# Two attention layers on one core: their chunks taken in turns, scores in groups of three, projections in 64x64 tiles

## The chip, the cores and the metric

The kernel runs on one core of one Trainium2 chip. The time is the device time of one execution, in microseconds (us); the kernel before takes 3326.32 us (median of 3 runs, 3324.19 to 3328.06).

## The reference

Eight images of 64 channels and 64 x 64 = 4096 positions go through two self-attention layers. Everything is fp32.

```python
# layer 0 (f and g have 8 channels, hh has 64)
f, g, hh = Wf @ xf + bf, Wg @ xf + bg, Wh @ xf + bh
s = jnp.einsum('bci,bcj->bij', f, g)
o = jnp.einsum('bcj,bij->bci', hh, jax.nn.softmax(s, axis=2))
x = x + o
# layer 1 (64 channels, one head)
xn = group_norm(x, 8 groups, gamma, beta)
q, k, v = split(w_qkv @ xn + b_qkv)
attn = softmax(einsum('bqc,bkc->bqk', q, k) * 64**-0.5)
out = w_proj @ (attn @ v) + b_proj + x
```

## The kernel before

An image is held as 128 partitions (64 channels of each half of the positions) by 2048 columns. An attention is worked in four **chunks** of 512 query columns, and a chunk in 16 **steps**. A step has two **blocks**: the scores of one block go into a score buffer in PSUM (there are three), the exponential takes them to SBUF, and the weighting matmuls of the step before add to an accumulator. VectorE sums the exponentials for the softmax denominator.

```python
for s in range(nsteps):                      # 4 chunks x 16 steps, one image, one layer
    for p in range(2):                       # two blocks
        ps = ps_s.tile([P, 2, CW], F32, tag="s", ...)      # 3 buffers
        for h in range(2):
            at.scores(ps[:, h, :], t, p, h, c)
    ...
        nc.scalar.activation(e[:, p], pss[p], AF.Exp, scale=at.scale)
    if ready is not None:
        weigh(*ready)                        # the step before
    ... units of the next attention's projections, finishing of the last chunk
```

The weighting of layer 0: two matmuls, one for each half `h`, use 128 rows and 64 columns of the array each. (In the trace each of these fp32 matmuls stands as two instructions: 4096 for 2048 calls. "Instructions" below are those of the trace.)

```python
# Layer0
def weigh(self, acc, e, t, p, start, stop):
    for h in range(2):
        nc.tensor.matmul(
            acc[0][ts(h, C), :], self.vt[:, p, t, :], e[:, h, :], start=start, stop=stop)
```

Layer 1 uses four 64x64 tiles at once for scores and weighting. The projections of layer 0 (f, g) and layer 1 (q, k) are full-width matmuls with zero or repeated weights. Attentions follow each other whole: layer 0 of image b, then layer 1 of image b-1.

Of the kernel before, what the change touches and what calls it, by code (L numbers as in the profile page):

```python
# [68 lines left out]
def fast_path(  # L69
# [13 lines left out]

    nc = tc.nc
# [9 lines left out]
    xpool = ctx.enter_context(tc.tile_pool(name="xpool", bufs=4))  # L94
    proj = ctx.enter_context(tc.tile_pool(name="proj", bufs=2))
    ppool = ctx.enter_context(tc.tile_pool(name="ppool", bufs=6))
# [23 lines left out]
    def zeros(name):  # L120
        t = const.tile([P, P], F32, name=name)
        nc.vector.memset(t, 0.0)
        return t
# [9 lines left out]
    wf, wg = zeros("wf"), zeros("wg")  # L133
    fb = const.tile([P, 1], F32, name="fb")
    gb = const.tile([P, 1], F32, name="gb")

    lane = const.tile([P, 1], I32, name="lane")
    nc.gpsimd.iota(lane, pattern=[[0, 1]], base=0, channel_multiplier=1)

    def low_rows(name, bit):  # L140
        hit = const.tile([P, 1], I32, name=f"{name}_bit")
        nc.vector.tensor_single_scalar(hit, lane, bit, op=ALU.bitwise_and)
        t = const.tile([P, 1], F32, name=name)
        nc.vector.tensor_scalar(t, hit, -1.0 / bit, None, op0=ALU.mult)
        return t

    fmask, gmask = low_rows("fmask", 2 * C8), low_rows("gmask", C8)
    for h in range(2):
        for p in range(2):
            r = 2 * h + p  # L150
            for j in range(4):
                rows = ds(32 * r + C8 * j, C8)
                nc.sync.dma_start(wf[ts(h, C), rows], WfT)
                nc.scalar.dma_start(wg[ts(p, C), rows], WgT)
                nc.gpsimd.dma_start(fb[rows, :], column(bf))
                nc.gpsimd.dma_start(gb[rows, :], column(bg))
    wh = diagonal("wh", WhT)
    hb = both("hb", bh)
    load_x(1)
# [3 lines left out]
    ones = const.tile([P, C], F32, name="ones")  # L163
# [4 lines left out]
    for h in range(2):  # L168
# [13 lines left out]
    stash = const.tile([P, 2 * B * NC * 2 * CW // P], F32, name="stash")  # L182
    recips = [
        dram.tile([P, 2 * CW // P], F32, name=f"recips_{i}") for i in range(2 * B * NC)
    ]

    def layer1_constants():


        wq = diagonal("wq", WqkvT[:, 0:C])  # L190
        wk = const.tile([P, 2, C], F32, name="wk")
        for p in range(2):
            for h in range(2):
                nc.gpsimd.dma_start(wk[ts(p, C), h, :], WqkvT[:, C : 2 * C])
        wp = diagonal("wp", WpT)
        wv = const.tile([C, C], F32, name="wv")
        nc.gpsimd.dma_start(wv, WqkvT[:, 2 * C : 3 * C])
        qb = both("qb", bqkv[0:C])
        kb = both("kb", bqkv[C : 2 * C])
        vb = both("vb", bqkv[2 * C : 3 * C])  # L200
        pb = both("pb", bp)
        gam = both("gam", gamma)
        bet = both("bet", beta)

        t0 = ps_s.tile([P, 2, CW], F32, tag="s", name="c_ps0")
        nc.tensor.transpose(t0[:C, 0, 0:C], wv, ident[0:C, 0:C])
        wvt = const.tile([C, 2, C], F32, name="wvt")
        for h in range(2):
            nc.vector.tensor_copy(wvt[:, h, :], t0[:C, 0, 0:C])
        t1 = ps_s.tile([P, 2, CW], F32, tag="s", name="c_ps1")  # L210
        nc.tensor.matmul(
            t1[:, 0, 0:C], wvt.rearrange("m h c -> m (h c)"), wp[0:C, 0:C], start=True, stop=True
        )
        wvp = zeros("wvp")
        for h in range(2):
            nc.vector.tensor_copy(wvp[ts(h, C), ts(h, C)], t1[ts(h, C), 0, 0:C])
        t2 = ps_s.tile([P, 2, CW], F32, tag="s", name="c_ps2")
        nc.tensor.matmul(t2[:, 0, 0:1], wvp, bet, start=True, stop=False)
        nc.tensor.matmul(t2[:, 0, 0:1], wp, vb, start=False, stop=True)
        nc.tensor.matmul(t2[:, 1, 0:1], wq, bet, start=True, stop=True)  # L220
        pbe = const.tile([P, 1], F32, name="pbe")
        nc.vector.tensor_add(pbe, t2[:, 0, 0:1], pb)
        qbe = const.tile([P, 1], F32, name="qbe")
        nc.vector.tensor_add(qbe, t2[:, 1, 0:1], qb)
        t3 = ps_s.tile([P, 2, CW], F32, tag="s", name="c_ps3")
        nc.tensor.matmul(
            t3[:, 0, 0:1], wk[0:C, :, :].rearrange("m h c -> m (h c)"), bet[0:C, :],
            start=True, stop=True,
        )
        kbe = const.tile([P, 1], F32, name="kbe")  # L230
        nc.vector.tensor_add(kbe, t3[:, 0, 0:1], kb)
        return wq, wk, gam, wvp, pbe, qbe, kbe


    def values(vt, src, w, c, name):

        ps = ps_s.tile([P, 2, CW], F32, tag="s", name=name)
        for t in range(TPC):
            nc.tensor.matmul(ps[:, 0, ts(t, P)], src[:, ts(t, P)], w, start=True, stop=True)  # L239
        nc.vector.tensor_copy(  # L240
            vt[:, :, ts(c, TPC), :],
            ps[:, 0, :].rearrange("k (t p c) -> k p t c", p=2, c=C),
        )

    class Attention:
        def __init__(self, index, b):
            self.index, self.b, self.name = index, b, f"l{self.kind}_{b}"

        def finish(self, acc, esum, c):

            n = f"{self.name}_{c}"
            raw = self.total(acc, n)
            zt = small.tile([P, 2 * CW // P], F32, tag="zt", name=f"zt_{n}")
            r = work.tile([P, CW], F32, tag="r", name=f"r_{n}")

            def sums():
                z = ps_s.tile([P, 2, CW], F32, tag="s", name=f"z_{n}")
                for h in range(2):
                    nc.tensor.matmul(  # L259
                        z[ts(h, C), 0, :], ones, esum[:, h, :], start=True, stop=True  # L260
                    )
                zs = work.tile([P, CW], F32, tag="zs", name=f"zs_{n}")
                nc.scalar.copy(zs, z[:, 0, :])  # L263
                for h in range(2):
                    nc.sync.dma_start(zt[ts(h, C), :], zs[h * C : h * C + 1, :])

            def reciprocals():
                dealt = recips[self.index * NC + c]
                rt = stash[:, ts(self.index * NC + c, 2 * CW // P)]
                nc.vector.reciprocal(rt, zt)  # L270
                nc.sync.dma_start(dealt, rt)
                for h in range(2):
                    row = dealt[ts(h, C), :].rearrange("p e -> (p e)")
                    nc.sync.dma_start(r[ts(h, C), :], row.partition_broadcast(C))

            def result():
                nc.vector.tensor_mul(raw, raw, r)  # L277
                self.residual(raw, c)

            return [(2, sums), (4, reciprocals), (8, result)]  # L280

    class Layer0(Attention):
        kind = 0
        banks = 1
        scale = 1.0

        def before(self):
            fg = proj.tile([P, 2, NH], F32R, tag="kfg", name=f"fg_{self.name}")
            self.f, self.g = fg[:, 0, :], fg[:, 1, :]
            self.vt = proj.tile([P, 2, NT, C], F32, tag="vt", name=f"vt_{self.name}")  # L290
            yield from (lambda c=c: self.project(c) for c in range(NC))

        def project(self, c):
            xc = x_tiles[self.b][:, ts(c, CW)]
            ps = ps_s.tile([P, 2, CW], F32, tag="s", name=f"fg_{self.name}_{c}")
            nc.tensor.matmul(ps[:, 0, :], wf, xc, start=True, stop=True)  # L296
            nc.tensor.matmul(ps[:, 1, :], wg, xc, start=True, stop=True)  # L297
            for i, (dst, bias, mask) in enumerate(((self.f, fb, fmask), (self.g, gb, gmask))):
                n = f"{i}_{self.name}_{c}"
                full = work.tile([P, CW], F32, tag="full", name=f"full{n}")  # L300
                nc.scalar.activation(full, ps[:, i, :], AF.Identity, bias=bias)  # L301
                high = work.tile([P, CW], F32R, tag="high", name=f"high{n}")
                nc.vector.tensor_copy(high, full)  # L303

                nc.vector.scalar_tensor_tensor(
                    dst[:, ts(c, CW)], high.bitcast(F32), mask, full,
                    op0=ALU.mult, op1=ALU.add,
                )
            values(self.vt, xc, wh, c, f"h_{self.name}_{c}")

        def scores(self, ps_ap, t, p, h, c):
            rows = ts(2 * h + p, 32)
            nc.tensor.matmul(  # L313
                ps_ap, self.g[rows, ts(t, P)], self.f[rows, ts(c, CW)], start=True, stop=True
            )

# [6 lines left out]
        def total(self, acc, n):  # L323
            raw = work.tile([P, CW], F32, tag="raw", name=f"raw_{n}")
            nc.scalar.copy(raw, acc[0])
# [565 lines left out]
```

## Time and profile before

| | before |
|---|---|
| median | 3326.32 us |
| TensorE busy | 3238.3 us, 97% |
| VectorE, ScalarE busy | 76%, 65% |
| an attention of layer 0, of layer 1 | 174, 236 us |
| first exponential starts | 43.67 us |

### The profile page before, as it was taken

How to read it: one execution, taken by the hardware profiler on the slowest of the kernel's cores; microseconds unless marked ns; L12 is line 12 of the kernel's file. 1: busy time of each engine (PE TensorE's matmuls, PEld its weight loads, DVE VectorE, ACT ScalarE, POOL GpSimd, SP SyncE). 2: the span in 40 equal slices, each digit the busy share in tenths (PEclk: the TensorE clock that was granted, in tenths of full speed). 3: DMA queues.
4: the chain of work that ended last, by engine and by line, in shares of the span. 5: the costliest groups of instructions: out<-in, count | busy, mean ns of one | idle time of the engine just before them, and what ended most of it. 6: DMA issues, size and time to landing. Idle time of an engine off the chain costs nothing.

```text
span 3324.7 us, 54178 instructions
## 1 busy us (share of the span) xinstructions
PE 3238.3 (97%) x23661; PEld 1109.9 (33%) x23661; DVE 2540.8 (76%) x1583; ACT 2170.2 (65%) x2329; POOL 33.2 (1%) x73
## 2 busy tenths in 40 slices
PE   6999999999999999999999999999999999999997
PEld 2323333333333333333333333332333323333332
DVE  5988866798667986678866798678876688766665
ACT  4778755687556765577655786557865577655554
POOL 3000000000000000000000000000000000000000
PEclk9999999999999999999999999999999999999999
DMA  2000000000000000000000000000000000000000
GB/s 54 7 7 7 8 7 11 23 7 7 8 14 20 7 8 7 14 20 7 8 8 14 23 4 7 12 9 10 7 4 14 8 10 7 4 14 7 14 8 15
DMA packets 42005, 37.90 MB, mean 11 GB/s; under 512 B 27248, under 2 KB 27424, under 8 KB 41760
## 3 DMA queue, kind: packets, MB, share of 16 engines
q1 hardware_dynamic: 38656, 34.14, 4.2%
q8 instruction: 187, 3.06, 0.4%
q0 software_dynamic: 1824, 0.19, 0.1%
q14 instruction: 58, 0.48, 0.0%
q10 hardware_dynamic: 1280, 0.03, 0.0%
HBM read 25.42 MB, written 8.65 MB: 10 GB/s over the span
## 4 chain that ended last, share of the span: by engine, by line
PE 82%; DVE 10%; DMA 3%; ACT 2%; issue 2%; POOL 1%; SPq 0%; DVEq 0%; ACTq 0%; POOLq 0%
PE s_l L391 27%; PE acc_l L399 26%; PE acc_l L319 19%; DVE esum_l L449 8%; PE s_l L313 5%; PE z_l L259 2%; ACT e_l L464 2%; DMA r_l<-recips 2%; DMA recips<-stash 1%; PE fg_l L296 1%; PE h_l L239 1%; PE fg_l L297 1%; PE k_l L379 1%; PE q_l L385 1%; PE v_l L239 0%
## 5 line engine op out<-in xcount | busy, mean ns | idle before, releaser
L464 ACT ACTIVATE e_l<-s_l 128x1024 f32<-128x1024 f32 x2048 | 1983.9, 1023 | 881.6 <-PE s_l L391 665.0
L449 DVE TENSOR_TENSOR esum_l<-esum_l,e_l 128x2048 f32<-128x2048 f32 x896 | 2051.6, 2290 | 414.4 <-ACT e_l L464 374.5
L319 PE MATMUL acc_l<-e_l,vt_l 128*64 128x512 f32 x4096 | 1010.4, 611 | 0.0
L391 PE MATMUL s_l<-q_l,k_l 64*64 64x512 f32 x8192 | 980.4, 591 | 0.0
L399 PE MATMUL acc_l<-e_l,vt_l 64*64 64x512 f32 x8192 | 976.4, 589 | 0.0
L399 PEld LDWEIGHTS acc_l<-e_l,vt_l 64*64 64x64 f32 x8192 | 318.4, 133 | 563.6 <-issue 454.7
L391 PEld LDWEIGHTS s_l<-q_l,k_l 64*64 64x64 f32 x8192 | 309.1, 133 | 566.0 <-issue 542.7
L319 PEld LDWEIGHTS acc_l<-e_l,vt_l 128*64 128x64 f32 x4096 | 252.4, 137 | 426.6 <-issue 410.7
L313 PE MATMUL s_l<-fg_l 32*128 32x512 f32 x2048 | 268.6, 499 | 17.5 <-ACT e_l L464 10.6
L313 PEld LDWEIGHTS s_l<-fg_l 32*128 32x128 f32 x2048 | 101.7, 183 | 412.6 <-issue 319.1
L449 DVE TENSOR_TENSOR esum_l<-e_l,e_l 128x2048 f32<-128x2048 f32 x64 | 146.7, 2291 | 76.8 <-ACT e_l L464 76.7
L277 DVE TENSOR_TENSOR raw_l<-raw_l,r_l 128x512 f32<-128x512 f32 x64 | 44.3, 693 | 122.6 <-DMA r_l<-recips 122.6
L263 ACT COPY zs_l<-z_l 128x512 f32<-128x512 f32 x64 | 37.5, 586 | 74.2 <-PE z_l L259 74.2
L451 DVE TENSOR_TENSOR esum_l<-esum_l 128x1024 f32<-128x1024 f32 x64 | 78.4, 1225 | 2.2
L259 PE MATMUL z_l<-esum_l,ones 128*64 128x512 f32 x256 | 67.9, 607 | 5.3 <-DVE esum_l L451 4.5
L270 DVE RECIPROCAL stash<-zt_l 128x8 f32<-128x8 f32 x64 | 12.8, 200 | 78.7 <-DMA zt_l<-zs_l 78.7
L301 ACT ACTIVATE full_l<-fg_l,fb 128x512 f32<-128x512 f32 x32 | 22.0, 687 | 77.7 <-PE fg_l L297 77.7
L303 DVE CAST high_l<-full_l 128x512 fp32r<-128x512 f32 x64 | 27.0, 422 | 41.1 <-ACT full_l L301 41.1
L383 ACT ACTIVATE k_l<-k_l,kbe 128x1024 f32<-128x1024 f32 x32 | 35.7, 1115 | 34.7 <-PE k_l L379 34.7
L296 PE MATMUL fg_l<-x,wf 128*128 128x512 f32 x64 | 36.6, 655 | 21.9 <-DMA wf<-in_WfT_dram 21.9
L409 DVE TENSOR_TENSOR raw_l<-acc_l,part_l 128x512 f32<-128x512 f32 x32 | 22.1, 690 | 25.6 <-ACT part_l L407 25.6
L407 ACT COPY part_l<-acc_l 128x512 f32<-128x512 f32 x32 | 18.7, 585 | 32.9 <-PE acc_l L399 32.9
(97 smaller groups left out, 629.2 us busy)
## 6 DMA issues: line engine op xcount, KB each, us to landing
r_l<-recips SPq DMA_DIRECT2D x128, 128.0 KB, 2.9
x<-in_x_dram SPq DMA_DIRECT2D x32, 256.0 KB, 4.9
out_dram<-raw_l SPq DMA_DIRECT2D x64, 128.0 KB, 2.4
zt_l<-zs_l SPq DMA_DIRECT2D x128, 2.0 KB, 1.8
recips<-stash SPq DMA_DIRECT2D x64, 4.0 KB, 1.4
wg<-in_WgT_dram ACTq DMA_DIRECT2D x16, 2.0 KB, 3.6
fb<-in_bf_dram POOLq DMA_DIRECT2D x16, 0.0 KB, 3.0
gb<-in_bg_dram POOLq DMA_DIRECT2D x16, 0.0 KB, 2.9
```

Of the source, the lines that this page charges most:

```text
L259: nc.tensor.matmul(z[ts(h, C), 0, :], ones, esum[:, h, :], start=True, stop=True)
L263: nc.scalar.copy(zs, z[:, 0, :])
L277: nc.vector.tensor_mul(raw, raw, r)
L296: nc.tensor.matmul(ps[:, 0, :], wf, xc, start=True, stop=True)
L313: nc.tensor.matmul(ps_ap, self.g[rows, ts(t, P)], self.f[rows, ts(c, CW)], start=True, stop=True)
L319: nc.tensor.matmul(acc[0][ts(h, C), :], self.vt[:, p, t, :], e[:, h, :], start=start, stop=stop)
L383: nc.scalar.activation(self.k[:, :, ts(c, CW)], ps, AF.Identity, bias=kbe)
L391: nc.tensor.matmul(ps_ap[ts(m, C), :], self.k[ts(h, C), p, ds(t * P + m * C, C)], self.q[ts(h, C), ts(c, CW)], start=True, stop=True,)
L399: nc.tensor.matmul(acc[m][ts(h, C), :], self.vt[ts(m, C), p, t, :], e[ts(m, C), h, :], start=start, stop=stop,)
L449: nc.vector.tensor_add(esum, first if t == 1 else esum, e)
L451: nc.vector.tensor_add(esum[:, 0], esum[:, 0], esum[:, 1])
L464: nc.scalar.activation(e[:, p], pss[p], AF.Exp, scale=at.scale)
```

## The change

The intent: relieve layer 0, where VectorE and TensorE are both nearly full, by letting its chunks alternate with those of layer 1; change tile shape less often (groups of three blocks); cut the cost of the projections; and start sooner. The diff, cut to its core:

```diff
+    lead = NC + 2                                  # six chunks of layer 0 first
+    seq = chunks0[:lead]
+    for i, one in enumerate(chunks1):              # then the layers take turns
+        seq.append(one)
+        seq.extend(chunks0[lead + i : lead + i + 1])
...
     class Layer0(Attention):
+        group = 3                                  # blocks scored together (Layer1: 2)
...
+            for j in range(2):                     # f and g of two chunks, 64x64 tiles
+                for h in range(2):
+                    nc.tensor.matmul(
+                        ps[ts(j, C), h, :], wfg[ts(h, C), :], xt[ts(h, C), ts(2 * k + j, CW)], ...)
+            # ... split in two parts, then 16 copies into the rows that the scores read
+                            nc.sync.dma_start(dst[rows, cols]..., split[...])
...
     class Layer0(Attention): def residual(self, o, c):
+            nc.vector.bn_stats(self.st[:, c, :], xc)        # statistics by chunk
...
     class Layer1(Attention): def before(self):
+            # steps of the chunk ahead of the image's first one
+            return [(0, channels), (2, means), (4, deviations), (6, begin)] + [
+                (6 + 2 * c, lambda c=c: self.project(c)) for c in range(1, NC)]
...
+            j = blocks[-1] + 1
+            now = i * NT + j // 2 - 1
+            run_until(now)                         # inserted work: row sums, projections, statistics
+            for r in ready:
+                weigh(*r, now)                     # weighting of the group before
```

Also in it: four loads of weights at the start in place of 32, layer 1's constants moved into the loop, the square root of the statistics by integer start value and four Newton steps on VectorE, row sums in four 128x32 tiles (which drops VectorE's half-sum), seven buffers of exponentials for six, three image buffers for four, one half of each key copied by DMA, and the finishing of a layer-0 chunk put off until the layer-1 chunk after it has run.

## The prediction

> **What bounds the kernel now.** I read the page's busy shares first, then two stage windows, then the order of time inside each stage, and the start last.
>
> The page puts TensorE at 97%, but the stages differ. In the busy times by stretch (us, busy of PE, weight loads, VectorE, ScalarE), the first row is one attention of layer 1, the second one of layer 0:
>
> ```profile
> PE 3238.3 (97%) x23661; PEld 1109.9 (33%) x23661; DVE 2540.8 (76%) x1583; ACT 2170.2 (65%) x2329; POOL 33.2 (1%) x73
> ...
> 1205.00:1441.00 236.00, 235.23 (x2108) 85.13 (x2100) 165.42 (x103) 133.23 (x143) 0.00 (x0) 1.00 0.04 9
> ...
> 1031.00:1205.00 174.00, 168.00 (x856) 52.80 (x858) 151.48 (x93) 137.77 (x148) 0.00 (x0) 0.99 0.06 15
> ```
>
> Layer 1 is solid TensorE, with VectorE idle for 71 us of 236. Layer 0 has TensorE and VectorE both nearly full. The timeline shows one step (two blocks of scores, their weighting) of layer 0 on TensorE, then its sums on VectorE:
>
> ```profile
> 1092.03 0.51 PE L313 MATMUL s_l<-fg_l 32*128 32x512 f32 x4
> 1092.47 1.94 PE L319 MATMUL acc_l<-e_l,vt_l 128*64 128x512 f32 x8
> ...
> 1094.34 0.50 PE L313 MATMUL s_l<-fg_l 32*128 32x512 f32 x4
> ...
> 1096.10 11.86 DVE L449 TENSOR_TENSOR esum_l<-esum_l,e_l 128x2048 f32<-128x2048 f32 x5
> ```
>
> A layer 0 step takes TensorE 2.30 us from start to start (0.44 scores, 1.87 weighting). Five sums take 11.86 us, one 2.29 (the page's mean), so they start (11.86 - 2.29) / 4 = 2.39 apart. Sixteen steps make a chunk: 38.3 us of VectorE for sums alone, 36.8 of TensorE. To this VectorE adds projections, statistics and residuals, 43 us in all per chunk, which is what a chunk takes (174 / 4 = 43.5). A layer 1 step (16 score and 16 weighting matmuls of 1.72 us each) takes 3.43, a chunk 54.9, and with projections and row sums 59 (236 / 4).
>
> The start, from the timeline and the chain: sixteen weight loads on each of two queues, then the projections, then layer 1's constants; the first score matmul comes at 42.8.
>
> ```profile
> 1.25 11.38 ACTq L154 DMA_DIRECT2D wg<-in_WgT_dram  x16
> ...
> 8.42 11.21 SPq L153 DMA_DIRECT2D wf<-in_WfT_dram  x16
> ...
> 21.85 2.05 PE L296 MATMUL fg_l<-x,wf 128*128 128x512 f32 x2 [21.85 <-DMA wf<-in_WfT_dram]
> ```
>
> I split TensorE's time into streaming and changes of tile shape. One pass of 512 columns takes 0.215 us, four passes for fp32, one for the rounded fp32 of layer 0's scores. In the program order of before I count 2966 us of streaming and 1195 changes of shape. From start to start a change costs 0.10 to 0.22 us: 8 weighting matmuls take 1.87 before scores, though 16 of the other layer stream for 1.72. The changes sum to 212. 2966 + 212 = 3178, less 11 at the start; the loop lasts 3324.7 - 42.8 - 19 (tail) = 3263. So about 97 us are stalls, 9 or 10 in each attention of layer 0 and under 1 in each of layer 1.
>
> **What the skill says.** The Trainium skill, "TensorEngine Tiling (Array Packing)", section Tiling Modes, says that a change of tiling mode (not of tile) drains TensorE; the 0.10 to 0.22 us above agree. Its page "ScalarE: Activation LUTs", section What ACT_TABLE_LOAD costs, gives about 1283 ns for a table load; the trace has 16 of 1283 ns in the loop, for the square root, 20.6 us of ScalarE. They go, but ScalarE is at 65%. "DMA: Bandwidth & Descriptors", section Rules for kernel authors, advises issuing a transfer early and waiting late; the copies of f, g and k do this, except at the start.
>
> **The change part by part.**
>
> *Projections in 64x64 tiles.* Before, f and g took 4 instructions of 0.43 us a chunk, 1.72; after, one group of four concurrent tiles (0.86) serves two chunks. 32 x (1.72 - 0.43) = 41 us. q and k go from 1.72 to 0.86: 32 x 0.86 = 27 us. Streaming falls by 69.
>
> *Groups of three.* Scores and weighting change shape 11 times a chunk, not 16. But a third block uses row groups that the first holds, so it can't run beside it. Where before had three blocks in a row, six matmuls took 0.73 us against 0.50 for four:
>
> ```profile
> 1030.82 0.73 PE L313 MATMUL s_l<-fg_l 32*128 32x512 f32 x6
> ```
>
> A group costs 0.65 + 2.58 + 0.15 = 3.38 us; ten and one group of two make 36.05 a chunk against 36.8. Over all: +34 us of streaming, fewer changes. In the order of after I count 1091 changes of all kinds, 179 us, and 2933 of streaming: 3112 against 3178. **TensorE's work falls by 66 us.**
>
> *Turns.* VectorE is what held layer 0, so its lag may now run into a layer 1 chunk, where it gains 1.04 us a step (3.43 - 2.39). Seven buffers of exponentials, of which the groups hold about three, allow some 10 us of lag. With both layers' finishing work (5.4 us) VectorE has 43.7 in a layer 0 chunk, TensorE 36.05 + 2.2 for row sums = 38.25: a lag of 5.5, which fits. A plain pair costs 38.25 + 55.2 + about 1 = 94.5.
>
> *Where turns don't help.* Six chunks of layer 0 come first, alone. VectorE holds them: 40.9 each, 48 with the next image's projection, 51 with layer 1's: 258 in all. And all of a layer 1 image's statistics and projections fall in one layer 0 chunk. There TensorE waits in order for the normalised x, which VectorE makes after six sums and some 30 small operations, near 24 us into the chunk; TensorE arrives near 20. Then queries, keys, values and scores share three score buffers, some 4 us more. I walk it to 54 us against 47.6 of TensorE's work. Six such chunks lie among the pairs: 6 x 15.75 = 94.5 above plain. Six layer 0 projections add 7.7 each, 46.
>
> *Start.* Four weight loads, not sixteen; layer 1's constants move into the loop. First matmul near 8.5, scaled copies to 13.7; six copies at some 0.57 us of issue (as two small loads take 1.15), plus 2.2 to land: first exponential near 20, not 43.7. A gain of 23.
>
> *Off the path.* The dropped half-sum (64 x 1.225 = 78 us) and the casts spare VectorE; layer 1's extra eviction costs ScalarE 32 x 0.585 = 19. Neither is a bound in a pair.
>
> *Sum.* 20 start + 258 lead + 26 x 94.5 = 2457 pairs + 94.5 + 46 + 347 for the last six layer 1 chunks (56.3 each, one image's projection 8, leftovers) + 19 tail = 3241.5. I put it at **3238 us**.
>
> **The rivals.**
>
> A. *VectorE and the score buffers give the stalls back.* If TensorE stops for each inserted matmul, because a group of three fills all three score buffers, each layer 0 chunk loses 2 us more, 26 pairs 52 us: about 3290. For it: each row sum now needs a buffer that an exponential must free. Against it: the order of after shows weighting matmuls ahead of most inserted ones, which fill that time.
>
> B. *The turns remove the stalls wholly.* Then 3112 + 39 (start, tail) + a few for the lead: about 3165. For it: layer 0's stalls are VectorE's, and a pair has slack on it. Against it: the lead has no layer 1 to lean on, and the projection chunk makes TensorE wait for VectorE in order.
>
> C. *The copies come late.* 256 copies of 64 KB for f and g, 64 of 128 KB for k, all issued by SyncE, some 9 us of issue per 16. If the queue blocks behind a reciprocal or a load of x, scores wait for keys, perhaps 5 us an image: 3280. Against it: each is used a chunk later, and DMA was at 3 to 7% in these stretches.
>
> D. *Groups of three starve TensorE.* Three exponentials (starts 0.92 apart) end 3.4 us after the scores begin, against a cycle of 3.38. So it holds barely; 0.2 us a group would be 352 x 0.2 = 70 us: above 3300.
>
> **Range and chances.** The floor is B, 3165, which I doubt by the lead alone, so the low end is 3185. A or C gives 3280 to 3290. Two per cent faster is 3326.3 x 0.98 = 3259.8, only 22 us above my figure, and my stalls (about 105 us) are the soft part. Faster 0.64, same 0.33, slower 0.03.
>
> **What would show each step.** TensorE's busy time falls by some 60 to 70 us. The first score matmul starts near 19 to 22 us. Six score matmuls and the 12 weighting instructions after them recur every 3.4 us in plain layer 0 chunks. A layer 0 chunk plus a layer 1 chunk takes 94 to 96 us where nothing is projected, and a layer 0 chunk with layer 1's projections 52 to 56, with TensorE waiting there for the normalised x. VectorE's lag shows as sums of layer 0 running after layer 1's scores have begun; its busy share is near 76%. I am wrong if plain pairs take 97 or more (A or D), if the projection chunk takes under 49 (towards B), if scores wait for a copy (C), or if the square of projections in 64x64 tiles does not run four at once.

## More of the kernel before

All runs quoted were fast ones. Every experiment was timed together with runs of the kernel before on the same chip. The chip differs from round to round, and with it the median of the kernel before, from 3323.99 to 3327.84 us; a difference between runs of different rounds is good to some 4 us.

A row has line, engine, operation, output <- input, shape and count, then busy time in us and mean ns of one, then idle time ahead of them with its releasers. The weighting of layer 0 and the full-width projections that the change replaces:

```profile
L319 PE MATMUL acc_l<-e_l,vt_l 128*64 128x512 f32 x4096 | 1010.4, 611 | 0.0
...
L296 PE MATMUL fg_l<-x,wf 128*128 128x512 f32 x64 | 36.6, 655 | 21.9 <-DMA wf<-in_WfT_dram 21.9
L379 PE MATMUL k_l<-xn_l,wk 64*128 64x512 f32 x128 | 36.1, 641 | 0.0
L385 PE MATMUL q_l<-xn_l,wq 128*128 128x512 f32 x64 | 36.0, 644 | 0.0
...
L297 PE MATMUL fg_l<-x,wg 128*128 128x512 f32 x64 | 33.6, 607 | 0.0
```

The four projection rows add up to 142.3 us. For the weighting, an instruction and its partner of the other half `h` can lie side by side in the array; 2048 such pairs in 1010.4 us are 0.49 us a pair, although one instruction alone takes 0.61: nearly all pairs run side by side. I counted in the trace the layer-0 weighting instructions whose partner does not start within 100 ns of them: 28 of 4096. I call these **lone** starts.

## The result, and the profile after

| | before | after |
|---|---|---|
| median | 3326.03 us (4 runs, one more than above) | 3332.19 us (4 runs, 3330.87 to 3336.0) |
| ratio, 95% interval | | 1.002, 1.0003 to 1.0038 |
| first exponential starts | 43.67 us | 21.53 us |
| lone starts of layer-0 weighting | 28 | 352 |

A ratio is the mean time of one kernel's fast runs over that of the other's of the same rounds, so it is not quite the ratio of the medians quoted. The change gains nothing. The start came as predicted and TensorE's busy time, which was to fall by 60 to 70 us, rose by 20:

```profile
PE 3258.4 (98%) x23985; PEld 1101.7 (33%) x23985; DVE 2442.2 (73%) x1591; ACT 2127.5 (64%) x2321; POOL 16.8 (1%) x41
```

The groups of the changed kernel that answer to those of before:

```profile
L364 PE MATMUL acc_l<-e_l,vt_l 128*64 128x512 f32 x4096 | 1055.6, 603 | 0.0
L357 PE MATMUL s_l<-fg_l 32*128 32x512 f32 x2048 | 271.2, 474 | 16.6 <-ACT e_l L567 13.7 <-DMA fg_l<-split_l 2.0 <-DVE vt_l L251 0.3
...
L444 PE MATMUL qk_l<-xn_l,wqk 64*64 64x512 f32 x256 | 42.1, 732 | 22.0 <-DVE xn_l L436 20.1 <-ACT e_l L567 1.8
...
L329 PE MATMUL fg_l<-x,wfg 64*64 64x512 f32 x128 | 18.3, 652 | 9.8 <-DVE low L150 9.8
```

The projections did shrink, from 142.3 to 18.3 + 42.1 = 60.4 us. The same 4096 weighting instructions cost 45 us more. And TensorE waits 20.1 us for the normalised x in 7 places, because the statistics stand just ahead of the projections. That wait is not new in size: the kernel before waited 20.9 us in 8 places inside the statistics (`gn_l` for `v_l`), and seven of these waits too were followed by a half-clock stretch, of 3.4 or 6.8 us. The change moved the loss and did not remove it.

**Why the weighting costs more.** TensorE's timeline of the changed kernel at the beginning of a layer-0 chunk (start, length of the run in us, line, operation, shape, count, and in brackets the idle time before):

```profile
1178.28 0.51 PE L357 MATMUL s_l<-fg_l 32*128 32x512 f32 x4
1179.19 0.49 PE L357 MATMUL s_l<-fg_l 32*128 32x512 f32 x2 [0.41 <-ACT e_l L567]
1179.67 1.07 PE L364 MATMUL acc_l<-e_l,vt_l 128*64 128x512 f32 x2
1181.09 1.06 PE L269 MATMUL z_l<-esum_l,ones 128*32 128x512 f32 x8 [0.34 <-ACT e_l L567]
1182.09 2.79 PE L364 MATMUL acc_l<-e_l,vt_l 128*64 128x512 f32 x10
1184.81 0.73 PE L357 MATMUL s_l<-fg_l 32*128 32x512 f32 x6
1185.47 2.80 PE L364 MATMUL acc_l<-e_l,vt_l 128*64 128x512 f32 x12
```

A group of three blocks has twelve weighting instructions, six pairs, in 2.80 us (last row). Where the row sums `z` are put in, the group is cut in 2 and 10. The ten take as long as the undisturbed twelve, and the two take 1.07 us, against 0.64 for one instruction. So two instructions (one matmul) stand ahead of `z` without their partners, and the partners stand alone behind it: four lone starts, two more time slots of 0.43 us. In the program `z` comes before all twelve. The scores have filled all three score buffers, `z` needs one and must wait for an exponential (0.34 us here); as I read the order, the scheduler, which orders each engine's instructions when the kernel is built, fills that time with a weighting matmul, without regard to the partner. A plain layer-0 chunk has two such places (eight lone starts in the chunk that starts at 1176.3).

**Why the chunk with layer 1's projections is long.** In the windows (core time, then busy us and counts of PE, weight loads, VectorE, ScalarE, GpSimd, then the granted clock, DMA share, GB/s) the first row is a plain layer-0 chunk, the second a plain layer-1 chunk, the third the layer-0 chunk that holds all projections of a layer-1 image:

```profile
1176.30:1218.20 41.90, 41.15 (x224) 12.36 (x226) 35.99 (x25) 32.32 (x36) 0.00 (x0) 1.00 0.08 20
1218.20:1273.00 54.80, 54.80 (x502) 19.04 (x494) 36.84 (x17) 31.60 (x33) 0.00 (x0) 1.00 0.01 1
1058.80:1121.50 62.70, 58.56 (x292) 20.50 (x294) 45.83 (x53) 40.38 (x49) 0.00 (x0) 0.92 0.20 47
```

The third row loses 4 us of idle TensorE, and its clock is 0.92. The timeline inside it, and the clock in 4 us stretches:

```profile
1086.07 1.38 PE L444 MATMUL qk_l<-xn_l,wqk 64*64 64x512 f32 x8 [3.04 <-DVE xn_l L436]
1087.37 2.08 PE L250 MATMUL v_l<-wvp,xn_l 128*128 128x128 f32 x8
1089.38 1.65 PE L357 MATMUL s_l<-fg_l 32*128 32x512 f32 x6
```

```profile
1083.00:1087.00 4.00, 0.95 (x10) 0.24 (x8) 3.17 (x13) 0.00 (x0) 0.00 (x0) 0.97 0.12 38
1087.00:1091.00 4.00, 3.94 (x18) 2.35 (x14) 1.51 (x3) 2.72 (x4) 0.00 (x0) 0.50 0.39 98
1091.00:1095.00 4.00, 3.74 (x20) 2.09 (x16) 3.10 (x3) 3.70 (x6) 0.00 (x0) 0.50 0.37 77
1095.00:1099.00 4.00, 4.00 (x16) 1.25 (x16) 3.35 (x3) 2.36 (x4) 0.00 (x0) 0.75 1.01 236
```

TensorE waits 3.04 us for VectorE, and then runs at half clock for some 10 us: six score matmuls take 1.65 us there against 0.73 above. Six of the seven such places in the changed kernel are followed by 6.8 or 10.2 us at half clock, one by 3.4. The Trainium skill describes this on its page "TensorE: Matmul & The Clock Gate", section HAM oscillation — how this bites in real kernels: an idle TensorE is throttled to half clock and the work after the wait starts there. The trace agrees: 3.04 us of wait, then 10.2 at half clock. I had not used it for the prediction.

### The profile page after: what moved, and what is told of

It reads as the page before. It is cut to its first block, busy times and chain, and to the rows that moved or that the text cites. A ratio compares the mean times of both kernels' runs of the same rounds, so it can differ in the third digit from the quotient of the medians.

```text
span 3334.3 us, 55600 instructions
## 1 busy us (share of the span) xinstructions
PE 3258.4 (98%) x23985; PEld 1101.7 (33%) x23985; DVE 2442.2 (73%) x1591; ACT 2127.5 (64%) x2321; POOL 16.8 (1%) x41
## 4 chain that ended last, share of the span: by engine, by line
PE 91%; ACT 4%; issue 2%; DVE 2%; SPq 1%; DMA 1%; ACTq 0%; DVEq 0%
PE acc_l L364 28%; PE s_l L464 26%; PE acc_l L472 25%; PE s_l L357 6%; ACT e_l L567 3%; PE v_l L250 2%; PE z_l L269 2%; PE qk_l L444 1%; SPq L349 1%; ACT raw_l L261 1%; DVE esum_l L539 1%; PE fg_l L329 0%; DMA fg_l<-split_l 0%; DVE split_l L339 0%; DMA x<-in_x_dram 0%
## 5 line engine op out<-in xcount | busy, mean ns | idle before, releaser
L364 PE MATMUL acc_l<-e_l,vt_l 128*64 128x512 f32 x4096 | 1055.6, 603 | 0.0
L464 PE MATMUL s_l<-kq_l 64*64 64x512 f32 x8192 | 973.9, 590 | 0.9 <-DVE vt_l L251 0.9
L464 PEld LDWEIGHTS s_l<-kq_l 64*64 64x64 f32 x8192 | 307.7, 133 | 581.5 <-issue 575.5
L451 ACT ACTIVATE kq_l<-qk_l,kbe 64x512 f32<-64x512 f32 x64 | 43.7, 682 | 51.6 <-PE qk_l L444 50.3
L269 PE MATMUL z_l<-esum_l,ones 128*32 128x512 f32 x512 | 69.2, 604 | 7.1 <-ACT e_l L567 6.9
L251 DVE COPY vt_l<-v_l 128x512 f32<-128x512 f32 x64 | 43.9, 687 | 39.0 <-PE v_l L250 39.0
L261 ACT COPY raw_l<-acc_l 128x512 f32<-128x512 f32 x96 | 53.9, 606 | 26.0 <-PE acc_l L364 20.7
L444 PE MATMUL qk_l<-xn_l,wqk 64*64 64x512 f32 x256 | 42.1, 732 | 22.0 <-DVE xn_l L436 20.1
L250 PEld LDWEIGHTS v_l<-wvp,xn_l 128*128 128x128 f32 x256 | 39.8, 237 | 32.6 <-ACT e_l L567 25.1
L274 ACT COPY zs_l<-z_l 128x512 f32<-128x512 f32 x64 | 39.8, 622 | 12.4 <-PE z_l L269 12.4
L250 PE MATMUL v_l<-wvp,xn_l 128*128 128x128 f32 x256 | 46.7, 338 | 0.0
L339 DVE SCALAR_TENSOR_TENSOR split_l<-high_l,lowmask,full_l 128x1024 fp32r<-128x1024 f32 x16 | 20.5, 1283 | 35.2 <-DMA fg_l<-split_l 34.9
```

Of the source, the lines that this page charges most:

```text
L250: nc.tensor.matmul(ps[:, 0, ts(t, P)], src[:, ts(t, P)], w, start=True, stop=True)
L251: nc.vector.tensor_copy(self.vt[:, :, ts(c, TPC), :], ps[:, 0, :].rearrange("k (t p c) -> k p t c", p=2, c=C),)
L261: nc.scalar.copy(raw[:, m, :], bank)
L269: nc.tensor.matmul(z[ts(2 * h + p, 32), 0, :], ones, esum[:, p, h, :], start=True, stop=True, tile_position=(0, 32 * (2 * h + p)),)
L364: nc.tensor.matmul(acc[0][ts(h, C), :], self.vt[:, p, t, :], e[:, h, :], start=start, stop=stop)
L444: nc.tensor.matmul(ps[ts(h if i == 0 else 1 - h, C), i, :], k1["wqk"][ts(h, C), i, :], xn[ts(h, C), :], start=True, stop=True,)
```

## The experiments

Two theories, for two separate losses. **P**: cut pairs cost the time in the layer-0 chunks. **H**: the normalised x comes late, and the half clock after the wait adds to it. Rivals: groups of three starve TensorE by themselves (rival D of the prediction); the three score buffers are too few for projections, values and scores; inserted work costs as much wherever it is put. The three runs without turns ask whether the turns are worth having at all.

The medians and ratios, with plain layer-0 chunk, the mean of the six projection chunks (starts of exponentials in the trace), and lone starts:

| kernel | median, us | ratio to before, 95% interval | plain | projection | lone |
|---|---|---|---|---|---|
| after | 3332.19 | 1.002 (1.0003 to 1.0038) | 41.9 | 61.5 | 352 |
| pairs kept | 3281.16 | 0.9866 (0.9849 to 0.9882) | 40.2 | 60.0 | 0 |
| inserted work after weighting | 3344.92 | 1.0058 (1.0042 to 1.0075) | 40.6 | 62.0 | 128 |
| groups of two | 3276.31 | 0.9852 (0.9836 to 0.9869) | 39.8 | 60.5 | 60 |
| pairs kept, groups of two | 3271.69 | 0.9837 (0.982 to 0.9853) | 39.8 | 59.8 | 0 |
| early statistics | 3299.49 | 0.9923 (0.9907 to 0.994) | 41.9 | 54.8 | 376 |
| pairs kept, groups of three, early statistics | 3241.21 | 0.9744 (0.9729 to 0.9759) | 40.2 | 52.4 | 0 |
| pairs kept, groups of two, early statistics | 3217.42 | 0.9678 (0.9662 to 0.9694) | 39.8 | 49.9 | 0 |

### Pairs kept

The second matmul of a pair gets priority and must follow the first; nothing else changes.

```diff
+            first = nc.tensor.matmul(acc[0][ts(0, C), :], ..., e[:, 0, :], ...)
+            with tc.high_priority():
+                second = nc.tensor.matmul(acc[0][ts(1, C), :], ..., e[:, 1, :], ...)
+            tc.add_manual_dep(second.ins, first.ins.name, <order only, no semaphore>)
```

> The changed kernel, with the two weighting matmuls of a layer 0 block (the two column tiles) tied together so that nothing comes between them in TensorE's order; all else as it was. Theory P (split pairs): in the trace of the changed kernel 352 weighting instructions of layer 0 start alone, 28 in the kernel before; a pair costs 0.43 us and a lone one also 0.43, so the split costs (352 - 28) / 2 x 0.43 = 70 us. Then this runs at about 3332 - 75 = 3257 us, a plain layer 0 chunk at 40.2 instead of 41.9 us, and lone starts fall to under 10. Rival Q (VectorE and the score buffers): TensorE would wait anyway for the buffers at those places, and the lone matmuls only filled the waits; then it stays at 3320 to 3335, with TensorE's waits for exponentials grown by some 70 us.

It took 3281.16 us, 51 less than the changed kernel. Its two rows of layer-0 weighting (one line for each half now) cover the same time, 977.2 us each, where the changed kernel's one row has 1055.6:

```profile
L363 PE MATMUL acc_l<-e_l,vt_l 128*64 128x512 f32 x2048 | 977.2, 605 | 0.0
L367 PE MATMUL acc_l<-e_l,vt_l 128*64 128x512 f32 x2048 | 977.2, 605 | 0.0
```

The plain chunk fell by 1.7 us, which is what its eight lone starts cost: 8 / 2 x 0.43 = 1.72. Over all lone starts the same sum gives 352 / 2 x 0.43 = 76 us, of which 51 came (55.7 between the two profiled runs: 35 in the 20 plain chunks, 12 in the lead, 9 in the projection chunks). The weighting's busy time did fall by 75, to 980.2 for both rows together, but TensorE then waited longer: for the normalised x 25.2 us in place of 20.1, for copies of the values (`vt_l`) 9.1 in place of 0.3. The projection chunk, with 20 lone starts in the one at 1058.8, fell by only 1.5. So P holds, and the size expected was half again too large.

### Inserted work after the weighting

```diff
-            run_until(now)
             for r in ready:
                 weigh(*r, now)
+            run_until(now)
```

> The changed kernel, with the inserted work (row sums, projections, statistics) issued after the weighting of the last group instead of before it, as the kernel before did. In its order the splits by inserted work are gone, but 62 weighting matmuls are still cut by scores of the next group. Theory P: lone starts fall from 352 to about 130, so 110 x 0.43 = 48 us less: 3284. Rival Q: what the inserted work waits for is not changed by its place, so 3320 or more; it could even be slower if statistics and projections now come later and meet the next chunk.

It took 3344.92 us, more than the changed kernel, and P's 3284 was missed by 61, although only 128 lone starts are left. In the plain chunks P holds here too: none of them has a lone start, and they fell from 41.9 to 40.6. What was gained there was lost elsewhere, most of it in the layer-1 chunk with layer 0's projections, which rose from some 62 to 68. The waits (us in total, times, longest) show why:

```profile
PE qk_l L444 <- DVE xn_l L436: 24.8, 7, 4.0
PE s_l L464 <- DVE vt_l L251: 20.9, 7, 3.6
```

The scores now stand right behind the projections and wait for the score buffers that these hold, 20.9 us in layer 1, where the changed kernel waits 0.9. Where projections are inserted, putting them ahead of the weighting was right.

### Groups of two, with and without kept pairs

```diff
     class Layer0(Attention):
-        group = 3
+        group = 2
```

> The changed kernel with layer 0's scores in groups of two blocks instead of three; turns, tiles and statistics stay. One score buffer is then free for inserted work, and the order shows only 30 cut pairs of 120. Theory P: about 260 fewer lone starts, 56 us less, and 5 more changes of shape in each of 32 chunks, 0.75 us a chunk, 24 us more: about 3300 us. Rival D of the prediction (groups of three starve TensorE): the same sign but larger, below 3280. If groups of three are a gain as intended, it is slower than 3332.

> Both: groups of two and pairs tied together. Theory P: cutting is gone, so it differs from the first of these runs by the changes of shape alone, 32 x 0.75 = 24 us more: about 3281 if that one runs at 3257. If it is faster than the first, the three full score buffers cost more than the changes of shape save, beyond the cut pairs (rival A of the prediction).

They took 3276.31 and 3271.69 us. The first is below the 3300 that P gave and in the range of rival D; the second is faster than groups of three with kept pairs, as rival A has it. The 24 us that more changes of shape were to cost did not show. With two blocks one score buffer stays free, inserted work need not wait for an exponential, and most cuts vanish by themselves (60 lone starts). With the pairs kept in both, groups of two are 9.5 us faster than groups of three here and 24 us faster once the statistics are early (3241.21 and 3217.42, below). Groups of three are therefore a small loss in themselves, and a large one through the cuts. Rival D's mechanism, TensorE starved group after group, is not what the trace shows: in the changed kernel 266 of the 305 groups of six score matmuls are followed by weighting after some 0.66 us. Most of the delayed ones are the first group of a layer-0 chunk, which takes 1.4 us: its third block waits 0.41 us for an exponential to free the third score buffer (the row at 1179.19 above). With kept pairs TensorE waits 14.6 us in all for exponentials before layer 0's scores in groups of three, and 0.9 in groups of two. That is rival A's cause, at the change of chunks.

### Statistics one chunk earlier

The small operations of the statistics of images 1 to 6 go ten steps earlier, into the layer-1 chunk before the projection chunk. The projections stay where they are. First on the changed kernel, then on the one with pairs kept and groups of two.

```diff
+            ahead = 10 if 0 < self.b < B - 1 else 0
-            return [(0, channels), (2, means), (4, deviations), (6, begin)] + [
+            return [(0 - ahead, channels), (2 - ahead, means), (4 - ahead, deviations), (6, begin)] + [
```

> The changed kernel with one thing moved: the statistics of images 1 to 6 of layer 1 are issued one chunk earlier, in the layer-1 chunk before their projection chunk, so that VectorE has the normalised x ready when the projections want it. Theory H (the projection chunk is long because TensorE waits for the normalised x and then runs at half clock): the chunk of 60.6 to 62.7 us falls to 54 to 56, the 20 us of waits for the normalised x nearly vanish, the half-clock slices at six of the seven places vanish, and the kernel falls by 6 times 5 to 7 us to some 3290 to 3302. The cut pairs stay (some 350 lone starts). Rival: the chunk is long because projections, values and scores share three score buffers; then the chunk stays above 59 and the kernel stays within 10 us of 3332.

> Pairs kept and groups of two (the kernel that took 3271.69) with the same early statistics. Theory H: its projection chunk of 58.4 us falls to 53 to 55, the wait of up to 6.6 us for the normalised x vanishes, and the kernel takes 3238 to 3250, which is six times 4 to 6 us less. Rival (shared score buffers): 3265 to 3275.

Alone it took 3299.49 us, 33 less than the changed kernel, inside the range of H. The same projection chunk, and what is left of the wait:

```profile
1053.20:1108.00 54.80, 54.03 (x288) 17.93 (x290) 42.35 (x32) 40.10 (x48) 0.00 (x0) 1.00 0.23 54
```

```profile
PE qk_l L445 <- DVE xn_l L437: 1.9, 1, 1.9
```

The clock is 1.00, and the clock record of this run has no half-clock stretch between the start and the end. The chunk fell from 62.7 to 54.8: 3.4 us of it idle time, 4.5 us busy time that had run slow. The rival of too few score buffers would have kept it above 59.

On top of kept pairs and groups of two it gave more than expected, 54 us (3271.69 to 3217.42): the chunk fell from 59.8 to 49.9, 6 x 9.9 = 59, less about 1 us in each chunk that now holds the statistics. The wait there had been longer (38.5 us in 7 places, up to 6.6) than in the changed kernel (20.1, up to 3.0): in the chunk at 1031.3 there TensorE arrives 20.5 us into the chunk and x is ready at 26.0, in the changed kernel's chunk at 1058.8 at 24.2 and 27.3. A TensorE that is not slowed waits longer for a late x.

### Both repairs with groups of three

Kept pairs and early statistics, nothing else undone. This run is the test of the whole account of the miss.

> As the best so far (3217.42), but layer 0 scores in groups of three again. It tells what groups of three cost where no pair is cut and the statistics are early. From the two earlier runs with pairs kept (plain layer-0 chunk 40.2 against 39.8) I expect 25 to 30 such chunks times 0.4 plus some 3 us in the lead: 3228 to 3235. If groups of three were a gain once the rest is mended (fewer changes of shape), it would be under 3215.

It took 3241.21 us, 91 less than the changed kernel, 6 above the range expected here, and 3 from the 3238 that I had predicted for the changed kernel. That closeness is partly luck: 26 plain pairs take 40.2 + 54.8 = 95.0 each, 13 us more than predicted in all, and the six projection chunks 52.4, where I had priced a wait for x that the early statistics remove; they are 21 us less above plain than predicted. TensorE's busy time is 3165.9 us, 72 less than in the kernel before, where the prediction had 60 to 70 less. Groups of three thus cost some 22 to 24 us against the 3217.42 of groups of two.

### Two attempts to go on from there

Projections spread over two chunks, on the version of 3217.42 us:

```diff
-            ] + [(6 + 2 * c, lambda c=c: self.project(c)) for c in range(1, NC)]
+                (11, lambda: self.project(1)),
+                (NT + 3, lambda: self.project(2)), (NT + 6, lambda: self.project(3))]
```

> As the run before with early statistics, pairs kept and groups of two, but the projections are spread: two in the projection chunk, two in the first layer-1 chunk of the image. If the copies and bias work of four projections in one chunk still crowd the score buffers, this gains a further 5 to 20 us (3225 to 3240). If nothing crowds any more, it equals the run before within 5 us.

It took 3223.18 us. The projection chunk fell to 46 to 48, and the next layer-1 chunk rose from 54.8 to 59.0: the work moved and there was no gain. (The difference of 5.8 us is just over the 5 allowed.)

The statistics of image 0 three steps earlier as well (`ahead = 3` there):

> The best so far (3217.42: pairs kept, groups of two, statistics of images 1 to 6 early) with the statistics of image 0 three steps earlier as well. Its projection chunk there is 58.0 us against 49.9 for the other images. Theory H (the normalised x comes late): three steps are about 7 us, so that chunk falls to 50 to 54 and the kernel to 3209 to 3214. Rival: the lead is bound by VectorE alone, the sums then lag by as much as is gained, and the kernel stays within 3 us of 3217.

It took 3218.72 us: no gain. The projection chunk fell from 58.0 to 52.4, and the layer-0 chunk before it rose from 37.8 to 43.0. In the lead there is no layer-1 chunk that could take the wait.

### Without turns

Pairs kept and groups of two, but whole images follow each other as in the kernel before:

```diff
-    seq = chunks0[:lead]
-    for i, one in enumerate(chunks1):
-        seq.append(one)
-        seq.extend(chunks0[lead + i : lead + i + 1])
+    seq = chunks0[: 2 * NC]
+    for b in range(B):
+        seq.extend(chunks1[b * NC : (b + 1) * NC])
+        seq.extend(chunks0[(b + 2) * NC : (b + 3) * NC])
```

> Pairs kept and groups of two, but the chunks of the two layers do not take turns: whole images follow one another as in the kernel before. It tells what the turns are worth. My theory that layer 0 alone is bound by the work of VectorE and the exponentials and that turns relieve it: its layer-0 chunks stay at 42 to 44 us and the kernel takes 3320 to 3350, some 60 us more than 3271.69. Rival: the gain of the kept pairs and smaller projections is all there is, and turns are worth less than 20 us: 3260 to 3290.

It took 3303.93 us, 32 more than with turns, and neither theory got it right. My theory had layer 0 bound by VectorE. But a plain layer-0 chunk among its like, in the first row below, takes 37.80 us with TensorE busy for all of it, and VectorE for 35.86. The loss is elsewhere, in the layer-1 chunk with layer 0's projections, second row, 72.9 us against some 62 with turns:

```profile
1045.00:1082.80 37.80, 37.80 (x202) 10.95 (x202) 35.86 (x20) 31.87 (x34) 0.00 (x0) 1.00 0.03 8
521.50:594.40 72.90, 64.55 (x568) 23.53 (x564) 42.20 (x29) 34.60 (x37) 0.00 (x0) 0.95 0.15 37
```

There SyncE issues 16 copies of f and g ahead of a copy of reciprocals, and VectorE waits in order for the latter (timelines of SyncE's queue and of VectorE, same run):

```profile
552.18 10.55 SPq L349 DMA_DIRECT2D fg_l<-split_l  x16
562.83 0.53 SPq L286 DMA_DIRECT2D recips<-stash  x1
```

```profile
567.99 0.69 DVE L294 TENSOR_TENSOR raw_l<-raw_l,r_l 128x512 f32<-128x512 f32 x1 [9.52 <-DMA r_l<-recips]
```

So I gave the early statistics to this order, and let the finishing of a chunk come four steps later:

> The best so far (3217.42: pairs kept, groups of two, early statistics) without turns, whole images one after the other, and with the finishing of a chunk four steps later, so that VectorE doesn't wait for the copies of the reciprocals, which cost the earlier run without turns (3303.93) some 8 us at each image. It tells what the turns are worth once nothing else stands in the way. Theory N (plain chunks cost the same in either order, 37.8 + 56.1 = 93.9 against 39.8 + 54.8 = 94.6, so turns by themselves are worth nothing): 3205 to 3230. Rival (turns give VectorE the room for projections and statistics): the layer-0 chunks with projections stay at 54 to 57 and the kernel takes 3245 to 3275.

It took 3266.46 us, in the range of the rival, but not for its reason: the layer-0 chunk with the projections fell to 48 us, and the layer-1 chunk stayed at 73 to 74. VectorE waited 140.3 us for the reciprocals' copies, after 138.5 in the first run without turns: later finishing had not removed the wait. So the next run moved the copies themselves:

```diff
-            return [(3, begin), (5, lambda: self.project(1))] + [
-                (7 + 2 * c, lambda c=c: self.values(...)) for c in range(NC)]
+            return [(-4, begin), (10, lambda: self.project(1))] + [
+                (s, lambda c=c: self.values(...)) for c, s in enumerate((-2, 0, 2, 12))]
```

> As the last run (no turns, 3266.46), whose layer-1 chunk with layer 0's projections still took 73 to 74 us: there the copies of f and g, the row sums' copies and the reciprocals' copies are all issued by SyncE in the same ten steps, and VectorE waits in order. Here the projections of layer 0 are moved out of those steps: the first at four steps before the chunk, the second ten steps into it, the values around them, the finishing as in the changed kernel. Theory N (turns are worth nothing by themselves): that chunk falls from 73.5 to 62 to 64, six to seven times ten us, and the kernel takes 3190 to 3210, under the 3217.42 of the best with turns. Rival (a collision of this kind comes back elsewhere and turns are what avoids it): above 3225.

It took **3199.25 us** (5 runs, 3196.34 to 3200.17), ratio 0.962 (0.9606 to 0.9633): the fastest kernel, 3.8% faster than the kernel before. Its stages, plain layer 0, plain layer 1, and the layer-1 chunk that had taken 73 us (layer 0's projections now begin in the chunk before it, which rose from 56.1 to 58.2):

```profile
1016.80:1054.60 37.80, 37.80 (x202) 10.94 (x202) 35.84 (x20) 31.88 (x34) 0.00 (x0) 1.00 0.03 8
1198.00:1254.10 56.10, 56.10 (x524) 19.67 (x520) 36.88 (x21) 32.51 (x35) 0.00 (x0) 1.00 0.04 11
918.40:978.60 60.20, 60.20 (x552) 22.28 (x548) 39.85 (x26) 33.46 (x36) 0.00 (x0) 1.00 0.13 31
```

A plain chunk of each layer costs 37.8 + 56.1 = 93.9 us without turns and 39.8 + 54.8 = 94.6 with them, at the same pairs and group size. The turns save nothing in plain chunks. What they did in the earlier comparison was to keep layer 0's copies away from layer 1's finishing, which another placement does too. One thing is left untested: the same placement of layer 0's projections with turns. As the chunk that holds them with turns shows under 1 us of idle TensorE (0.86 of 62.5 us at 487.0 in the run of 3217.42), I expect little of it.

## Why the prediction was wrong

The time, 3332 us, is outside the range of 3185 to 3290. Its own sum, term by term (us), with the profile of the changed kernel beside it:

| term | predicted | measured |
|---|---|---|
| start | 20 | 21.5 |
| lead of six layer-0 chunks | 258 | 272.3 |
| 26 pairs | 26 x 94.5 = 2457 | 26 x (41.9 + 54.8) = 2514 |
| projection chunks above plain | 6 x 15.75 = 94.5 | 6 x (61.5 - 41.9) = 118 |
| layer 0's projections | 6 x 7.7 = 46 | 6 x 7.0 = 42 |
| last six layer-1 chunks | 347 | 347 |
| tail | 19 | 19 |
| sum | 3241.5 | 3334 (profiled span 3334.3) |

- **Start: right.** First exponential at 21.5 for 20; the 22 us were gained in full.
- **Projections in 64x64 tiles: right.** The four tiles run at once: 69 us of streaming were to go, and the rows fell by 82 us of busy time (from 142.3 to 60.4, which includes what ran at half clock). The copies came in time, as expected against rival C: scores waited 2.0 us in all for them.
- **"TensorE's work falls by 66 us": this is the step that failed.** TensorE's busy time rose by 20 us (3238.3 to 3258.4). I counted 2933 us of streaming by taking every weighting instruction as half of a pair that runs side by side, in an order in which 352 of them no longer do. The order was there to be read before the run; I read which kinds of instruction come before which, and not whether partners stayed together. The run with kept pairs shows 51 us for it, most of it in plain chunks and the lead, and a busy time of 3187.7.
- **The projection chunk: mechanism right, size off, and one term missing.** I said that TensorE would wait there for the normalised x and put the chunk at 54 us; it was 61.5. TensorE came to the wait at 24.2 us and x at 27.3 in the chunk at 1058.8, for the 20 and 24 predicted: both 3 to 4 us late. The missing term is the half clock after the wait; cut pairs add a little. The run with early statistics shows 33 us for six chunks.
- With both mended and all else as changed, the kernel takes 3241.21 us. Outside the projection chunks the rest of the sum holds to within 13 us a term. One addition is off: the lead's own figures (four chunks of 40.9, 48 and 51) make 262.6, not 258; with kept pairs it took 260.2.
- **"VectorE is what held layer 0": wrong, though it did not move the sum much.** Layer 0's chunks run at 37.8 us without turns with TensorE never idle, once pairs are kept and groups have two blocks; I had put those of the lead at 40.9. The kernel before had shown it: TensorE was busy 168 of the 174 us of a layer-0 attention, VectorE 151. That is 37.9 us of VectorE a chunk, where the prediction says "43 us in all per chunk" under the very row. It also counts sixteen sums a chunk, 38.3 us; the page has 960 sums for 64 chunks, fifteen each, and at 2.29 us they take 34.4, less than TensorE's 36.8. So the turns had no bound to relieve in plain chunks. My sum got a plain pair right (94.5, measured 95.0 with pairs kept and groups of three) because TensorE's work was in it anyway.
- **Groups of three** were to cost 36.05 us a chunk in place of 36.8, a gain. They are a loss of 22 to 24 us with all else mended.
- **The rivals.** A was nearest: a group of three fills all three score buffers, and each layer-0 chunk does lose about 2 us. I had argued against it that weighting matmuls fill the time; they do, as halves of pairs, which is just the loss. D named 70 us and a delay in every group; groups of three do cost 22 to 24 us, but at the change of chunks. C did not happen. B was out of reach.

## What to carry to other kernels

Where two matmuls share the array, count in the final order of instructions how often a pair stays together, and tie the partners to each other if a scheduler may move them; half a pair costs as much as a whole one. Put the small serial work that a matmul depends on a stage early, into a stage in which its engine has time: a late operand costs the wait and then, in most places here, some microseconds at half clock. And before interleaving two stages to relieve an engine, check by the busy time of the other engines in that stage that it is the bound there.

## What the Trainium skill lacked or had wrong

- "TensorEngine Tiling (Array Packing)", Tiling Modes: it says that tiles operate independently, and that a change of mode drains. It doesn't warn that neighbours must stay neighbours in the order of instructions: ten instructions, two of them without their partners, took 2.79 us, the twelve of six whole pairs 2.80, and one cut pair of instructions costs 0.43 us. It also gives no size for the change of mode, 0.10 to 0.22 us here. "TensorE: Matmul & The Clock Gate", section Part 3: Packing small matmuls — row/col tiling, does say that matmuls are strictly first in, first out; that is half the warning, and the trace agrees: the partners behind `z` start 2.4 us after the instructions that they were cut from.
- "TensorE: Matmul & The Clock Gate", section HAM oscillation — how this bites in real kernels: it gives "no PE-idle gaps >~3.4µs" as its rule. Here seven waits in the changed kernel, one of 1.9 and six of 3.0 us, were each followed by 3.4 to 10.2 us at half clock. Others were not: 1.9 us in the run with early statistics, 2.3 in the one with both repairs and groups of three. So no single length of wait is a safe rule here.
- "DMA: Bandwidth & Descriptors", Issuing engines are not separate DMA queues: it calls the issue time usually small next to the transfer. In the run of 3303.93 us 16 copies of 64 KB took SyncE 10.55 us to issue, 0.66 each, where one takes 2.0 us from issue to landing (median): in a row on one queue they add up, and VectorE, which needed the result of a 4 KB copy queued behind them, waited 9.5 us.
